# Layer 1 of a two-layer decoder: the order in which the expert units' first loads are issued, and the pace of the routing steps beside the cross-attention

## The chip, the cores and the metric

The kernel runs on one core of one Trainium2 chip. A core has TensorE (PE, matmuls; its weight loads are shown as PEld), VectorE (DVE), ScalarE (ACT), GpSimd (POOL) and SyncE (SP). In this kernel SyncE issues nearly all block loads, and GpSimd issues the indirect DMAs that send or add rows by index. The metric is the device time of one execution in microseconds (us), as the median of several runs.

## What is computed

A batch of 32 sequences of 100 tokens, 256 wide, goes through two pre-norm decoder layers. Each layer has a self-attention, a cross-attention to a context of 361 rows of 128, and a mixture of experts, each added to the residual. Layer 1, which the change touches, is this in the reference (cut):

```python
x = x + _L1_attn_ref(_layernorm(x), ...)          # linear, masked, no softmax
x = x + _L1_xattn_ref(_layernorm(x), ctx_512, ...) # 16 heads of 64, softmax over 361
x = x + _L1_ffn_ref(_layernorm(x), ...)

# _L1_ffn_ref: T = 3200 tokens, E = 64 experts, K = 8, CAP = 256
scores = sigmoid(x @ gate_weight.T)
sfc = scores + e_bias
group_scores = top_k(sfc.reshape(T, 8, 8), 2)[0].sum(-1)
_, gidx = top_k(group_scores, 4)                   # 4 of 8 groups stay
tmp = where(group is kept, sfc, 0)
_, topk_idx = top_k(tmp, 8)
topk_w = scores at topk_idx, over their sum, times 2.5
# token t takes the next free place pos of each of its 8 experts; pos >= CAP is dropped
xe[e, pos] = x[t]
h = silu(xe @ w1.T) * (xe @ w3.T)                  # per expert, 128 wide
ye = h @ w2.T
out[t] = sum over its experts of topk_w * ye[e, pos]
out = out + (silu(x @ shared_gate.T) * (x @ shared_up.T)) @ shared_down.T
```

## The kernel before

The 3200 tokens are 25 tiles of 128 rows (`NF` = 25); the residual stays in SBUF for the whole program. The order of PE's instructions is written out by hand (`manual_schedule`); for the other engines a scheduler orders the program's instructions by their dependencies and by an estimate of when they can run. DMAs on SyncE's queue are issued in that queue's order, and an instruction that has to wait holds what stands behind it on its engine.

**Cross-attention of layer 1** (`xattn_stream`, L421 to L490). It runs over `NB` = 32 sequences in 4 steps each, a step being 4 heads: 128 steps `n`, software-pipelined. In each turn of the loop PE gets the scores of step n, then what `between(n)` puts in, then the turning (transposes, L455) of the exps of step n - 1, then one `tick`, then the values (L473) of step n - 2. `between` (L853 on) puts in the projections of keys, values and queries for what comes next, and, as soon as a tile of 128 rows is whole, that tile's output projection and its norm's statistics.

**Routing beside it.** The mixture's routing can be done for a group of tiles once they are projected. `ROUTED` gives the groups: three tiles each from tile 0, 3, ..., 18 on, then two from 21 on and two from 23 on. When a group's last tile is projected, `between` appends a generator `route(f, G)` (L1576 to L1693) to `self.routes`. Between two `yield`s it does one small portion:

- the normalised rows `xr` (L191, DVE), two tiles to a portion
- the turns: transposes of `xr` on PE (L213), their copy out of the PSUM bank to `xnT` by DVE or ACT in turns; again two tiles to a portion, so a group of three has two
- the gates' matmuls (L138 with `gw`) and the sigmoid on ACT (L1599)
- eight portions on DVE, from `sfc` (L1602) by `cnt`, `gm`, `tmp`, `eq`, `sel`, `tot` and `pp` (one matmul pair on PE) to `slot` (L1681), the places of the rows
- then 8 portions per tile of the kind `SEND`: one indirect DMA of GpSimd each (L1686), 128 rows from `xr` to `x_d` in HBM by `slot`

`tick` goes over all routes and advances each by one portion, but lets only one `SEND` go per tick. A step has one tick in `between` (L889) and one after the turn, until n > 116, where `between` makes two. Inside `between`, the loop over `ROUTED` reuses the name `n` in steps in which a tile is projected, so that these steps have one tick there. What a tick adds is made to follow the work of its step (`s.after`, `lay.after`), so that it isn't brought forward.

**The end of the stream.** `last_tile` runs after the last sequence: it projects the last tile, ticks until all earlier groups are through, then routes the last group. `list1` (L1695) makes from the counts a list of the experts in the order in which they are worked (`listf`, `listi`).

**The mixture of layer 1** (`l1_ffn`, L1750 on). PE first gets the remaining portions of the shared expert that are set ahead (about 25 us of them), called the filler below. A one-element memset on GpSimd, the flag (L1784), depends on all sends. Then `units` (L1855 on) goes over the experts in the order of the list, one unit each; for unit i:

- `weights(i)` (L1860): SyncE reads the expert's number from `listi` and issues one 384 KB load to `we` (12 buffers)
- `rows(i)` (L1866): SyncE reads the list again and issues the load of the expert's rows from `x_d` to `xe` (8 buffers); it depends on the flag
- `expert_turn(i)` (L1914): transposes of `xe`, copied by ACT to `xT`
- `expert_hidden(i-1)`: the two hidden matmuls, silu on ACT, product on DVE
- `expert_add(i-2)`: the matmul back, the weight per row, and the indirect DMA that adds the rows to a sum in HBM (L1956)

Nine weights and then five rows are issued ahead of the loop; in the loop each turn issues `rows(i+5)`, then `weights(i+9)`. At the end the sums are loaded, added to the residual and written out.

Of the kernel before, what the change touches and what calls it, by code (L numbers as in the profile page):

```python
# [17 lines left out]
NB = 32  # L18
# [47 lines left out]
def tile_of(b):  # L66

    f = tiles_before(b + 1)
    return f - 1 if f > tiles_before(b) else None
# [12 lines left out]
class Kernel:  # L82
# [706 lines left out]
    def l1_xattn(self):  # L789
        nc, tc, a = self.nc, self.tc, self.a  # L790
        self.route_begin()
        with ExitStack() as st:
# [7 lines left out]
            class Lay:  # L800
# [52 lines left out]
                def between(s, n, sums):  # L853
                    b, g = divmod(n, 4)

                    part, of = {3: (0, b), 1: (1, b - 1)}.get(g, (0, -1))
                    if 0 <= of < NB:
                        r = pool.tile([T, 8], F32, tag="r", name="r")
                        nc.vector.reciprocal(r, sums[of][:, 8 * part : 8 * part + 8])
                        by_row = me.by_row(pool, r, 4)  # L860
                    if n + 1 < 4 * NB:
                        s.keys(n + 1)
                    if b < NB:
                        for c in ((0, 1), (2,))[g % 2]:
                            s.vals(b, g // 2, c)
                        if g == 0 and b + 2 < NB:
                            s.load(b + 2)
                        if b % 2 and b + 1 < NB:
                            s.queries(b + 1, 2 * g)

                    if g == 1 and 0 < b < 5:
                        f = 16 + 2 * b
                        n = min(2, NF - f)
                        me.norm_turn(f, n, me.norm_rows(f, n, bias=me.xbo1), me.bank_p())
                    if b == NB and g < 2:

                        if g == 0:
                            me.shared = me.shared1(pool.tile([P, 8, 2 * T], F32, tag="qT", name="qT"))
                        next(me.shared)
                    if b == NB and g == 2:  # L880
                        s.last_tile()
                    elif g == 2 and b > 0 and tile_of(b - 1) is not None:
                        f = tile_of(b - 1)
                        me.out_proj(f, wo)
                        me.norm_stats(f, ROUTED)
                        for f0, n in ROUTED.items():
                            if f0 + n == f + 1:
                                me.routes.append([me.route(f0, n), None])
                    for _ in range(1 + (n > 4 * NB - 12) if n < 4 * NB + 2 else 0):  # L889
                        me.tick(s.after)  # L890
                    if 0 <= of < NB:
                        s.rT = me.row_scale(pool, by_row)
# [863 lines left out]
    def l1_ffn(self):  # L1756
        nc, tc, a = self.nc, self.tc, self.a
        x = self.x
        with ExitStack() as st:
# [26 lines left out]
            whole, first, second = (0, 1), (0,), (1,)  # L1786
            units = [(u, whole) for u in range(WHOLE)] + [(u, first) for u in range(WHOLE, UNITS)]
            end = self.units(ep, units, steps)
            n = nc.values_load(self.listi[0:1, 2 * E1 : 2 * E1 + 1], min_val=0, max_val=E1)
            with tc.If(n > 0):  # L1790
                units = [(u, second) for u in range(WHOLE, UNITS)] + [(u, whole) for u in range(UNITS, E1)]
                more = self.units(ep, units)

                word = pool.tile([1, 1], F32, tag="word", name="word")
                got = nc.sync.dma_start(word, self.sum_d[0][0:1, 0:1])
                self.depend(got, [more.ins], "the units' sums")
# [57 lines left out]
    def units(self, pool, units, beside=None):  # L1854

        nc, tc = self.nc, self.tc
        we, xes, xTs, hTs, added = {}, {}, {}, {}, {}
        n_all = len(units)

        def weights(i):  # L1860
            we[i] = pool.tile([P, 768], F32, tag="we", name="we", bufs=12)
            u = units[i][0]
            e = nc.sync.value_load(self.listi[0:1, E1 + u : E1 + u + 1], min_val=0, max_val=E1 - 1)
            nc.sync.dma_start(we[i], self.a["wexp"][bass.ds(e, 1)].rearrange("o p n -> p (o n)"))

        def rows(i):  # L1866
            u, halves = units[i]
            t = xes[i] = pool.tile([P, 2, XROW], F32, tag="xe", name="xe", bufs=8)
            e = nc.sync.value_load(self.listi[0:1, u : u + 1], min_val=0, max_val=E1)
            if len(halves) == 2:  # L1870
                at = self.x1_d.rearrange("(e s p) d -> e p s d", p=P, s=2)[bass.ds(e, 1)]
                got = nc.sync.dma_start(t, at.rearrange("o p s d -> p (o s) d"))
            else:
                at = self.x1_d.rearrange("(e s p) d -> s e p d", p=P, s=2)[halves[0]][bass.ds(e, 1)]
                got = nc.sync.dma_start(t[:, 0, :], at.rearrange("o p d -> p (o d)"))
            if beside:
                self.depend(got, [self.flag.ins], "all rows are in their places")

        with tc.manual_schedule(engines={mybir.EngineType.PE}):
            room = 0.0  # L1880
            for i in range(9):
                weights(i)
            for i in range(5):
                rows(i)
            for i in range(n_all + 2):
                if i + 5 < n_all:
                    rows(i + 5)
                if i + 9 < n_all:
                    weights(i + 9)
                if i < n_all:  # L1890
                    self.expert_turn(pool, i, len(units[i][1]), xes, xTs)
                if 0 <= i - 1 < n_all:
                    self.expert_hidden(pool, i - 1, len(units[i - 1][1]), we[i - 1], xTs, hTs)

                if beside and i > 2:
                    room = room + 1.0 if i < n_all else 100.0
                    while room > 0:
                        took = next(beside, None)
                        if took is None:
                            break  # L1900
                        room -= took
                if 0 <= i - 2:
                    self.expert_add(pool, i - 2, units[i - 2], we.pop(i - 2), xes, hTs, added, beside)
        flag = pool.tile([1, 1], F32, tag="flag", name="flag_u", bufs=2)
        flag = nc.gpsimd.memset(flag, 0.0)
        self.depend(flag, added[0] + added[1], "the units' sums")
        return flag
# [174 lines left out]
```

## Time and profile before

| what | us |
|---|---|
| runs shown: median (lowest to highest, 3 runs) | 3111.43 (3109.09 to 3111.95) |
| the profiled execution's own time | 3138.55 |
| its span on the core | 3136.8 |
| mean granted clock of TensorE in it | 0.982 of full speed |
| PE busy in the span | 3002.3 |
| 1862 to 2912 | cross-attention of layer 1, up to its last steps |
| 2912 to 2944 | last steps and last tile: PE busy 25.0 of 32.0, granted clock 0.84 |
| 2944 to 2980 | list, filler, start of the units: PE busy 27.9 of 36.0 |
| 3000 to 3020 | units: PE busy 20.0 of 20.0, DMA share 0.94 |

The profiled execution is 27 us, 0.9%, above the median of the runs; durations are read from it. In a row of a timeline the two numbers are the start in the span and the duration, then come the engine, the line of the source, the operation, and what it writes and reads; "x9" says that nine neighbours are put together, and the bracket gives the idle time of the engine before it and what ended it. Line numbers are those of the kernel before.

The sends before the flag are the pieces of GpSimd's work to look for: 200 of them, 0.97 us each, 194.5 us in all. A load of weights is 384 KB, a load of rows 321 KB on the mean.

### The profile page before, as it was taken

The numbers are of one execution on the slowest core, as the hardware profiler recorded it, in microseconds if no ns is written. First come the engines' busy times: TensorE is split into PE (matmuls) and PEld (weight loads), VectorE is DVE, ScalarE is ACT, GpSimd is POOL, SyncE is SP. The second block draws the span as 40 slices with busy tenths as digits, with TensorE's granted clock in tenths as the row PEclk, the third lists the DMA queues.
The fourth block names the chain that finished last, engine by engine and source line by source line (L and its number), as shares of the span: only waits on it lengthen the run. The fifth ranks groups of instructions, "written<-read, shape, count | busy, mean of one in ns | idle before, by whom it ended". The sixth has DMA issues, their size and how long they took to land. (4 is left out here: it accounts for less than half of the span.)

```text
span 3136.8 us, 67846 instructions
## 1 busy us (share of the span) xinstructions
PE 3002.3 (96%) x26802; PEld 2251.5 (72%) x26802; DVE 1806.7 (58%) x4686; ACT 1403.8 (45%) x4361; POOL 911.1 (29%) x1040
## 2 busy tenths in 40 slices
PE   8999999999999899999998999999999999999893
PEld 7777777677777658888874677777777777776483
DVE  6666665577777632222226876666676665766354
ACT  5555554566666511122222235545555555455120
POOL 3212221465555551000015520011212112122364
PEclk9999999999999999999998999999999999999997
DMA  8860000000000033545542000010000000000296
GB/s 311 295 212 1 1 1 1 17 16 14 15 14 14 16 123 136 189 180 191 209 162 63 19 5 6 6 37 21 25 9 10 12 8 15 7 11 4 70 223 192
DMA packets 127930, 224.55 MB, mean 72 GB/s; under 512 B 39373, under 2 KB 106245, under 8 KB 120816
## 3 DMA queue, kind: packets, MB, share of 16 engines
q1 hardware_dynamic: 97680, 126.00, 12.7%
q0 software_dynamic: 26640, 90.80, 8.8%
q8 instruction: 215, 3.52, 0.5%
q10 hardware_dynamic: 3280, 3.28, 0.3%
q14 instruction: 115, 0.94, 0.1%
HBM read 152.45 MB, written 112.56 MB: 84 GB/s over the span
## 5 line engine op out<-in xcount | busy, mean ns | idle before, releaser
L1686 POOL DMA_INDIRECT x_d<-xr,slot x200 | 194.5, 972 | 773.9 <-DVE kT L133 243.6
L446 ACT ACTIVATE wBx<-ps_t,m 100x361 f32<-100x361 f32 x512 | 280.8, 560 | 258.9 <-DVE m L443 233.2
L138 PE MATMUL ps_t<-xnT,wA 128*128 128x200 f32 (+1 forms) x1600 | 328.0, 349 | 1.5 <-DMA wA<-in_wq 0.9
L138 PEld LDWEIGHTS ps_t<-xnT,wA 128*128 128x128 f32 x1600 | 271.4, 192 | 50.5 <-issue 32.2
L443 DVE TENSOR_REDUCE m<-ps_t 100x1 f32<-100x361 f32 x512 | 241.0, 525 | 78.4 <-PE ps_t L138 76.3
L138 PE MATMUL ps_t<-xT,w 128*128 128x256 f32 x1276 | 283.2, 381 | 0.7 <-ACT xT L132 0.7
L138 PEld LDWEIGHTS ps_t<-xT,w 128*128 128x128 f32 x1276 | 240.0, 190 | 41.7 <-issue 9.3
L616 DVE TENSOR_REDUCE m<-ps_t 100x1 f32<-100x361 f32 x512 | 235.4, 517 | 18.1 <-PE ps_t L138 18.1
L637 ACT ACTIVATE e<-ps_t 121x300 f32<-121x300 f32 x512 | 173.9, 426 | 123.0 <-PE ps_t L138 123.0
L340 POOL TENSOR_TENSOR e<-e,rz 100x400 f32<-100x400 f32 x128 | 109.2, 854 | 407.6 <-DVE rz L339 393.0
L336 ACT ACTIVATE e<-s,m 100x100 f32<-100x100 f32 x512 | 186.1, 365 | 21.0 <-DVE m L330 20.3
L138 PE MATMUL ps_t<-cT,wA 128*128 128x361 f32 x512 | 188.5, 492 | 1.6 <-SPq L1285 1.6
L138 PE MATMUL ps_t<-kT,qT 64*100 64x361 f32 x1024 | 189.1, 485 | 0.9 <-ACT wBx L446 0.9
L641 POOL TENSOR_TENSOR es<-e 121x400 f32<-121x400 f32 x128 | 132.2, 1033 | 197.4 <-ACT e L637 197.2
L455 PEld LDWEIGHTS ps_t<-ident,wBx 100*121 100x121 f32 x1536 | 177.9, 186 | 12.6 <-issue 5.1
L138 PE MATMUL ps_t<-wA,cT 128*121 128x512 f32 x384 | 184.9, 593 | 0.8 <-ACT wBx L446 0.8
L455 PE MATMUL ps_t<-ident,wBx 100*121 100x100 f32 x1536 | 184.8, 269 | 0.0
L138 PE MATMUL ps_t<-wA,zT 128*128 128x256 f32 x784 | 181.5, 385 | 0.0
L1367 DVE TENSOR_TENSOR h<-ps_t,g 128x256 f32<-128x256 f32 x145 | 61.2, 424 | 199.4 <-ACT g L1366 199.4
L138 PEld LDWEIGHTS ps_t<-wA,zT 128*128 128x128 f32 x784 | 147.9, 191 | 27.7 <-issue 3.3
L133 DVE COPY eT<-ps_t 121x300 f32<-121x300 f32 x339 | 146.6, 461 | 30.4 <-PE ps_t L455 26.4
L473 PE MATMUL ps_z<-eT,v 121*64 121x100 f32 x3072 | 160.9, 254 | 0.0
(317 smaller groups left out, 5741.9 us busy)
## 6 DMA issues: line engine op xcount, KB each, us to landing
x_d<-fill SPq DMA_DIRECT2D x16, 1284.0 KB
we<-in_wexp SPq DMA_DIRECT2D x32, 384.0 KB
cT<-in_ctxT SPq DMA_DIRECT2D x64, 181.5 KB
xe_d<-zero SPq DMA_DIRECT2D x8, 1024.0 KB
xe<-x_d SPq DMA_DIRECT2D x24, 321.0 KB
xe<-xe_d SPq DMA_DIRECT2D x29, 256.0 KB
y_d<-y SPq DMA_DIRECT2D x29, 256.0 KB
sum<-fill SPq DMA_DIRECT2D x10, 640.0 KB
```

The source lines that it names most:

```text
L133: return self.nc.vector.tensor_copy(out, in_)
L138: self.nc.tensor.matmul(out, lhsT=l, rhs=r, start=(i == 0), stop=(i == n - 1))
L336: nc.scalar.activation(t[:, i, :], s[:, i, :], AF.Exp, bias=m[:, i : i + 1], accum_out=rz[:, i : i + 1])
L340: nc.gpsimd.tensor_tensor(t[:, h, :], t[:, h, :], self.last(rz[:, h], T), ALU.mult)
L443: lay.after = nc.vector.tensor_reduce(m, ps[i], AX.X, ALU.max, negate=True)
L446: nc.scalar.activation(t[:, :L], ps[i], AF.Exp, bias=m, accum_out=sums[b][:, h : h + 1])
L455: nc.tensor.transpose(pt[:, c, :], e[n, i][:, c * KC : (c + 1) * KC], self.ident[:T, :T])
L473: nc.tensor.matmul(out, lhsT=v, rhs=eT[n, i][:, c, :], start=first, stop=last)
L616: nc.vector.tensor_reduce(m[:, j, o : o + 1], ps[r], AX.X, ALU.max, negate=True)
L637: nc.scalar.activation(t[:, r], ps[r].rearrange("p (c t) -> p c t", c=NKC), AF.Exp)
L641: nc.gpsimd.tensor_tensor(s, t[:, :, 0, :], t[:, :, 1, :], ALU.add)
L1686: got = nc.gpsimd.indirect_dma_start(out=self.x1_d[:, :], out_offset=bass.IndirectOffsetOnAxis(ap=slot[:, j, k : k + 1], axis=0), in_=xr[: ...
```

## The change

```diff
@@ between(), in the cross-attention of layer 1 @@
-                    for _ in range(1 + (n > 4 * NB - 12) if n < 4 * NB + 2 else 0):
+                    for _ in range(1 + (n > 2 * NB) if n < 4 * NB + 2 else 0):
                         me.tick(s.after)
@@ units() @@
             room = 0.0
-            for i in range(9):
+
+            for i in range(5):
                 weights(i)
             for i in range(5):
                 rows(i)
+                if i < 4:
+                    weights(i + 5)
             for i in range(n_all + 2):
                 if i + 5 < n_all:
                     rows(i + 5)
                 if i + 9 < n_all:
                     weights(i + 9)
```

With `NB` = 32 the second tick of `between` now comes from step 65 on, where it came from step 117 on. In `units` the same nine weights and five rows are issued ahead of the loop, in the order w0 to w4, r0, w5, r1, w6, r2, w7, r3, w8, r4, where it was w0 to w8, r0 to r4. The later loads keep their order. `units` is also called in the branch for experts beyond the planned number of units (`n > 0` in `l1_ffn`), which is there in both kernels.

## The prediction

> **What bounds the kernel now.** I read the page's busy times and slices first, then the chain of waits, then the two places the change touches: the steps of layer 1's cross-attention in which a group of tiles is routed, and the stretch in which layer 1's units begin.
>
> ```profile
> PE 3002.3 (96%) x26802; PEld 2251.5 (72%) x26802; DVE 1806.7 (58%) x4686; ACT 1403.8 (45%) x4361; POOL 911.1 (29%) x1040
> PE   8999999999999899999998999999999999999893
> ```
>
> TensorE is busy for 96% of the span, and only the slices near the end show more than a tenth of idling. So a change can gain only in the dips, and it loses wherever it puts a wait in front of a matmul. Windows cut at the step boundaries (length, then busy time of PE, PEld, DVE, ACT, POOL, the granted clock, the DMA share and GB/s):
>
> ```profile
> 2395.30:2402.66 7.36, 7.36 (x62) 5.05 (x61) 5.10 (x13) 6.43 (x18) 1.83 (x2) 1.00 0.13 34
> 2402.66:2412.30 9.64, 9.64 (x75) 7.19 (x73) 5.67 (x13) 5.99 (x16) 2.33 (x3) 1.00 0.01 2
> 2412.30:2420.14 7.84, 7.84 (x64) 5.73 (x62) 6.87 (x29) 5.25 (x13) 1.55 (x2) 1.00 0.02 2
> 2420.14:2431.91 11.77, 11.77 (x79) 8.90 (x77) 9.07 (x37) 4.02 (x12) 1.16 (x2) 1.00 0.00 0
> ...
> 2848.50:2863.32 14.82, 12.01 (x75) 8.69 (x73) 6.27 (x17) 6.00 (x15) 2.58 (x3) 0.94 0.01 1
> ```
>
> The first four rows are steps 67 to 70, where the group of tiles from 9 on is routed: TensorE is never idle, so routing is free there today. The last row is step 122, in which the two-tile group from 21 on begins: this is the one place of the trace where routing already goes at more than two ticks a step, and PE loses 2.81 us of 14.82. Two rows of PE's timeline name its waits there:
>
> ```profile
> 2860.60 0.78 PE L213 MATMUL ps_t<-ident,xr 128*128 128x128 f32 x4 [2.81 <-DVE xr L191]
> ...
> 2875.94 1.12 PE L138 MATMUL ps_t<-wA,cT 128*121 128x512 f32 x2 [0.79 <-ACT wBx L446]
> ```
>
> Together 3.60 us for that group. At the start of the units, the timelines of SyncE, GpSimd and TensorE:
>
> ```profile
> 2953.25 18.59 SPq L1864 DMA_DIRECT2D we<-in_wexp  x9
> 2972.68 6.15 SPq L1872 DMA_DIRECT2D xe<-x_d  x6
> ```
>
> ```profile
> 2963.90 0.97 POOL L1686 DMA_INDIRECT x_d<-xr,slot  x1 [0.31 <-issue]
> 2966.45 0.09 POOL L1784 MEMSET flag<- 1x1 f32 x1 [1.58 <-DMA x_d<-xr,slot]
> ```
>
> ```profile
> 2974.45 1.03 PE L138 MATMUL ps_m<-wA,wB 128*128 128x256 f32 x4
> 2976.61 0.66 PE L1914 MATMUL ps_t<-ident,xe 128*128 128x128 f32 x4 [1.13 <-DMA xe<-x_d]
> 2977.89 0.66 PE L1914 MATMUL ps_t<-ident,xe 128*128 128x128 f32 x4 [0.62 <-DMA xe<-x_d]
> 2978.38 1.89 PE L138 MATMUL ps_s<-xT,we 128*128 128x256 f32 x8
> ```
>
> The flag (every row has been sent) is up at 2966.5, but SyncE is still issuing the nine weights and reaches the first rows only at 2972.68. They land 3.9 us later, and the first expert's hidden matmul starts at 2978.38. The shared expert's filler ends at 2974.45 + 1.03 = 2975.48.
>
> **Part one: the order on SyncE.** Nothing is added or removed: the same nine weights and five rows, in another order. The chain of waits shows that the first weights cost SyncE 2.8 to 4.2 us each while GpSimd sends (the fifth is issued at 2967.43), and 1.12 us each after that (2968.15, 2969.26, 2970.38, 2971.50). So the four weights that change places cost 4 x 1.12 = 4.5 us. First rows: 2972.68 - 4.5 = 2968.2, behind the flag. Second: two weights, not four, have been moved past when its own turn comes, since a weight now stands between: 2973.84 - 3 x 1.12 = 2970.5. The fifth is where it was. Landing by the old 3.9 us: 2972.1 and 2974.4, both before the filler's end.
>
> That gain isn't had in full, because the filler is in PE's order ahead of the first turn: the turn cannot start before 2975.48. Two turns back to back at the spacing of the rows above (2976.61 to 2977.89, of which 0.62 waits) take about 1.3 us with the copy that follows, so the hidden matmul starts at about 2976.8 in place of 2978.38: **-1.6 us**. From there on TensorE is busy in full (20.00 of 20.00 us in the windows from 3000 to 3020 and from 3040 to 3060), so an earlier start reaches the end one for one.
>
> Bounds: at best the rows go as the flag rises (2972.68 - 2966.6 = 6.1 us) and land faster than 3.9 us, at 7.2 us in all by a landing 1.1 us shorter; that needs the filler out of the way. At worst SyncE is through with the nine weights before the flag (as it would be at 1.12 us each from 2949 on, done by 2960). Then the first rows, which wait for the flag, hold four weights behind them on SyncE's queue, and the later rows come one to four slots later: +1.1 to +4.5 us. I take -1.6, nearest to the rows as they are.
>
> The Trainium skill ("Perfetto Trace Analysis", section "DMA Instruction — HWDGE (DVE, Sync)") says that the DMA engines do not wait for semaphores here; the sequencer's wait comes before descriptors are made. By that rule weights six to nine stand behind the flag, which speaks against this change; with the flag at 2966.45 and the fifth weight issued at 2967.43, the trace has nothing waiting, and the rule would make the sum +1.1 to +4.5 in place of -1.6 only if SyncE were faster.
>
> **Part two: two ticks from step 65 on.** Before, the second tick in `between` came only for n > 116. Groups up to the one from 6 on are routed before step 65 and stay. Following the generator tick by tick, the groups from 9, 12, 15 and 18 on (begun at n = 66, 82, 98, 110) change; the one from 21 on and the last, in `last_tile`, tick as they did. No instruction is added. For the group from 9 on: the first turn stays in step 67, the second follows in the same `between`, the gates' matmuls come in step 67 and not 68, the DVE part from `sfc` to `slot` fills steps 68 to 71 where it filled 68 to 72, and the 24 sends end in step 80 where they ended in 85. For the last of the four, sends end in 124 in place of 126. The final 16 sends are the last group's, in `last_tile`; so the flag does not move, and this part has **no gain** to give: PE has no idle time in steps 67 to 70 to win back, and a send on GpSimd (0.97 us) has room at 29% busy.
>
> What it can cost. Both turns and the gates now fall in one step. The gates need the copy of the second turn out of its bank; that copy is in a queue behind ACT's exps or DVE's copies. By hand, from the rows of step 67, PE reaches the gates at 2401.2 and the copy ends at 2401.7: 0.5 us. Then DVE: steps 68 and 69 hold 5.67 + 6.87 = 12.54 us of DVE work in 17.48 us, of which 3.5 us is routing; at two ticks in `between` and one after the turn it becomes about 8.4 us, which gives 17.4 of 17.48. DVE has no slack left in that stretch and runs late by some 2 us; the seven transposing banks cover most of it, and I leave 0.25 us for PE. Together 0.75 us a group, four groups: **+3.0 us**. Lower bound 0: TensorE is wholly busy there, which excludes a gain. Upper bound 3.60 us a group, from the two-tile group that already goes at this pace: 4 x 3.60 = +14.4. I take a value far below it because most of that row (2.81) is a turn that waits for its own rows' DVE work in the same step, and here the rows are made one step earlier. Only the 0.79 us row is of the kind I expect. What is late next after such a wait: every matmul, since PE is in order.
>
> **Sum.** -1.6 + 3.0 = +1.4 us on the profiled execution's 3138.55 (its span is 3136.8, with 1.75 around it): 3140. This execution lies 27.1 us above the median of the runs shown, 3111.43; the slow weight issues on SyncE may be part of that, and I carry the difference over unchanged: 3111.43 + 1.4 = 3112.8, **3113 us**. A measurement of this kernel can tell about 0.2%, 6.2 us, from no change.
>
> **The rivals.** *SyncE held at the flag* (chance 0.10): if SyncE is quicker in an unprofiled run, the wait takes the place of the nine weights, as bounded above: +3.0 + 1.1 to 4.5, so 3115.5 to 3119. For it: 2.8 to 4.2 us a weight is seen only while GpSimd sends back to back. Against it: weights six to nine are needed only by experts six to nine.
>
> *Three ticks a step stall TensorE* (slower, 0.31): the four three-tile groups each lose what the two-tile group loses, 3.60 us: 14.4 - 1.6 = +12.8, **3124 us**. It decides from (6.2 + 1.6) / 4 = 1.95 us a group. For it: the only group that runs so does lose that much, and DVE gets 17.4 us of work in 17.48. Against it: its 2.81 us has a cause that the bigger groups lack, and steps 117 to 121, which have the extra tick and only sends in it, show no wait.
>
> *The filler gives way* (faster, 0.18): if the filler's own waits in this stretch (2.86 us and 2.30 us of PE idling from 2959 to 2969) are short in an unprofiled run, PE asks for the rows by 2970.3, and the early rows are worth up to 7.2 us, with routing free: 3111.43 - 7.2 = **3104 us**. Against it: whatever shortens the filler would speed up SyncE's weights as well, and then less is left to gain.
>
> *The change does nothing that counts* is inside the forecast: 40-odd sends end earlier in the middle and nobody waits for them.
>
> **How the numbers follow.** Forecast 0.41, held at the flag 0.10, stall 0.31, filler gives way 0.18. The forecast's own range is 3109 to 3118 (-1.6 alone, up to +6). Of it 0.04 is beyond +6.2, of the held case 0.03. Slower 0.31 + 0.04 + 0.03 = 0.38; faster 0.18, less 0.01 for the part of it that stays within 6.2 us; the same 0.45. The range for all: 3102, a little below the best case, to 3125, just past the stall.
>
> **What would show it.** Right: rows first issued near 2968, the hidden matmul at about 2976.8, and PE idling of 0.5 us ahead of the gates in steps 67, 83, 99 and 111, with DVE near full in the two steps after. Wrong: PE waits of 2 us and more at L213 or at scores after those steps (stall); weight six issued a slot after the flag with PE waiting for rows two to four (held); the turn at L1914 following its filler by 2971 (gives way); or a flag that moves, which would make the tick count above wrong.

## The result, and the profile after

The changed kernel takes 3115.27 us (median of 20 runs, 3111.91 to 3120.24), the kernel before 3109.72 us (20 runs, 3106.59 to 3113.99). The ratio is 1.0017, with a 95% interval from 1.0011 to 1.0023: about 5.3 us longer (0.0017 x 3109.7), inside the 0.2% that were called the same, but clear of noise at this number of runs.

```profile
span 3112.3 us, 67848 instructions
PE 2990.1 (96%) x26802; PEld 2246.0 (72%) x26802; DVE 1806.7 (58%) x4687; ACT 1404.6 (45%) x4360; POOL 913.1 (29%) x1040
```

The profile after has a *shorter* span than the profile before (3136.8), though the kernel is slower. The experiments below ran in four batches, each with the kernel before beside it; that kernel takes 3109 to 3110 us in three of them and 3140 in one. The profile before looks like that one batch: SyncE needs 18.59 us in it for nine weights, 19.2 to 19.8 in two runs of that batch, and 9.69 in a batch at 3110. What sets the batch apart is not shown; it carries the same chip number, 3, as the first batch at 3110 us. So where an expectation below speaks of a chip at 3110 or 3140 us, a batch is all that was seen, and the two profiles are not subtracted here. What can be compared is a stretch, counted from a point in it; below that point is the start of the last matmul on the last group's counts (ps_t<-acc,ones), and the stretch is list, filler and units. The kernel with the old loads that is set beside it is the one of the second experiment (ticks only), which takes the time of the kernel before and was profiled in a batch where that is 3110 us.

**SyncE.** The change's timeline (start, duration, engine, line, operation):

```profile
2925.26 5.23 SPq L1864 DMA_DIRECT2D we<-in_wexp  x5
2941.24 0.39 SPq L1872 DMA_DIRECT2D xe<-x_d  x1
2942.39 0.33 SPq L1864 DMA_DIRECT2D we<-in_wexp  x1
2943.51 0.38 SPq L1872 DMA_DIRECT2D xe<-x_d  x1
```

and that of the old order:

```profile
2925.36 9.69 SPq L1864 DMA_DIRECT2D we<-in_wexp  x9
2941.29 6.16 SPq L1872 DMA_DIRECT2D xe<-x_d  x6
```

SyncE is not slow here: nine weights take 9.69 us, where the profile before showed 18.59. In both orders the first rows leave as the flag rises (2941.1), so the new order makes them no earlier. It leaves SyncE without work from 2930.5 to 2941.2, and the second rows leave 1.1 us later, since a weight stands between.

**TensorE and VectorE.** The change, TensorE's timeline from the filler's end on (the bracket is the idle time before it and what ended that):

```profile
2943.30 1.88 PE L138 MATMUL ps_t<-xnT,wA 128*128 128x512 f32 x4
2947.64 2.08 PE L138 MATMUL ps_m<-wA,wB 128*128 128x256 f32 x4 [2.46 <-DVE x_sb L1837]
2949.51 1.64 PE L1917 MATMUL ps_t<-ident,xe 128*128 128x128 f32 x8
2951.24 1.13 PE L138 MATMUL ps_s<-xT,we 128*128 128x256 f32 x4
```

The same with the old loads:

```profile
2943.45 1.88 PE L138 MATMUL ps_t<-xnT,wA 128*128 128x512 f32 x4
2945.17 1.03 PE L138 MATMUL ps_m<-wA,wB 128*128 128x256 f32 x4
2946.03 1.04 PE L1914 MATMUL ps_t<-ident,xe 128*128 128x128 f32 x8
2947.31 1.99 PE L138 MATMUL ps_s<-xT,we 128*128 128x256 f32 x8 [0.24 <-ACT xT L1918]
```

With the change TensorE stands still 2.46 us ahead of the filler's last four matmuls, waiting for an addition on VectorE, and then takes twice as long for them (2.08 against 1.03) and longer for the first turns (1.64 against 1.04). Together that is 2.46 + 1.05 + 0.60 = 4.1 us. Why VectorE was late shows in the change's chain of waits (start, duration, what):

```profile
2943.51 3.37 DMA xe<-x_d
...
2946.90 0.35 DVE one L1949
2947.25 0.34 DVE x_sb L1837
...
2947.64 2.08 PE ps_m L138 x4
```

and in VectorE's timeline, where `one` (L1949) is the units' weight per row:

```profile
2944.07 0.35 DVE L1949 SCALAR_TENSOR_TENSOR one<-io,listf,xe 128x128 f32<-128x128 f32 x1 [7.02 <-DMA xe<-x_d]
...
2944.66 0.68 DVE L1830 TENSOR_TENSOR wB<-ps_t,wB 128x512 f32<-128x512 f32 x1
2946.90 0.35 DVE L1949 SCALAR_TENSOR_TENSOR one<-io,listf,xe 128x128 f32<-128x128 f32 x1 [1.56 <-DMA xe<-x_d]
2947.17 0.42 DVE L1837 TENSOR_TENSOR x_sb<-ps_m,x_sb 128x256 f32<-128x256 f32 x1
```

VectorE waits 7.02 us for the first rows and 1.56 us for the second, with the filler's product (L1830) and additions (L1837), whose inputs are there, queued behind. Nothing in the diff touches VectorE. But VectorE's order is the scheduler's, and it followed the loads: VectorE's program order, before and after, ends the filler like this (`-` before, `+` after, line numbers of each):

```
 L1830 wB<-ps_t,wB            hidden product of the filler
 L1837 x_sb<-ps_m,x_sb  x2    additions of the filler
+L1949 one<-io,listf,xe       first unit: needs the first rows
+L1953 by<-one
 L1830 wB<-ps_t,wB            hidden product of the filler
-L1837 x_sb<-ps_m,x_sb  x2
-L1946 one<-io,listf,xe
-L1950 by<-one
-L1946 one<-io,listf,xe
+L1949 one<-io,listf,xe       second unit: needs the second rows
+L1837 x_sb<-ps_m,x_sb  x2    (with by<-one between the two)
 L1830 wB<-ps_t,wB            last hidden product of the filler
```

The loads of rows stand earlier in SyncE's order, the scheduler puts `one` earlier in VectorE's order in turn, and on the chip the rows do not come earlier, because the flag lets none go.

**The cross-attention.** PE's groups with any idle time in front of them, from 1862 to 2900, in the change:

```profile
L138 PE MATMUL ps_t<-wA,cT 128*121 128x512 f32 x360 | 174.6, 593 | 0.9 <-ACT wBx L446 0.9
...
L213 PE MATMUL ps_t<-ident,xr 128*128 128x128 f32 x46 | 7.7, 292 | 3.1 <-DVE xr L191 3.1
```

Both are the two-tile group's, as before (0.8 and 2.8 us there). The four groups that now go at two ticks a step cost TensorE nothing.

### The profile page after: what moved, and what is told of

Read it like the earlier page. It is cut to its first block, busy times and chain, and to the rows that moved or that the text cites. A ratio compares the mean times of both kernels' runs of the same rounds, so it can differ in the third digit from the quotient of the medians.

```text
span 3112.3 us, 67848 instructions
## 1 busy us (share of the span) xinstructions
PE 2990.1 (96%) x26802; PEld 2246.0 (72%) x26802; DVE 1806.7 (58%) x4687; ACT 1404.6 (45%) x4360; POOL 913.1 (29%) x1040
## 3 DMA queue, kind: packets, MB, share of 16 engines
q8 instruction: 215, 3.52, 0.5%
```

## The experiments

In all of them the ratio is to the kernel before, run beside it in the same batch on one chip, with its 95% interval. Runs of different batches are never set against each other by their times.

### One part at a time

```diff
# order only: units() as changed, between() as before
# ticks only: between() as changed, units() as before
```

> Only the new order of loads, the ticks as before. In the profile after, SyncE is through with five weights at 2930.5 and issues nothing until the flag (2941.1), and the DMA engines stand idle from about 2934 to 2941. Theory 'idle DMA time': four weights of 384 KB are moved out of that gap into a stretch where the DMA engines are 80 to 100% busy; at the 294 GB/s of the rows from 2951 to 2961 that is 4 x 384 / 294 = 5.2 us. It expects the whole loss here: +4 to +6 us on the kernel before. Theory 'ticks' (the loss is in the cross-attention): -1.6 to +1 us.

Measured: 1.0015 [1.0006, 1.0024], 3114.72 us beside 3109.86. The whole loss is in the order of the loads, and TensorE's wait is there too (2.78 us ahead of ps_m, for x_sb).

> Only the two ticks a step, the loads in the old order. Theory 'idle DMA time': nothing, -1 to +1 us, since TensorE's matmuls of the cross-attention stand at the same distances in both profiles. Theory 'ticks': +3 us or more, as the prediction summed it (0.75 us for each of four groups).

Measured: 0.9995 [0.9986, 1.0004], 3109.72 us beside 3109.86. The pace of the routing costs nothing and brings nothing; +3.0 us would be a ratio of 1.0010, outside the interval.

### The dose: rows first, and twelve weights ahead

```diff
+            for i in range(5):
+                weights(i)
             for i in range(5):
                 rows(i)
+            for i in range(5, 9):
+                weights(i)
```

> Five weights, then the five rows, then weights six to nine; ticks as before. The rows leave as early after the flag as in the kernel before, and still four weights stand behind the flag. Theory 'idle DMA time': as slow as the new order, +4 to +6 us. Theory 'late rows' (rows two to five come one to four slots of 1.1 us later because a weight stands between): no loss, -1 to +1 us.

Measured: 1.0012 [1.0003, 1.0022], 3115.25 us (5.4 more by the medians). This went as "idle DMA time" expected and against "late rows". But its timelines show what both had overlooked: VectorE stands 7.04 us at `one`, this time with three of them ahead of the filler's work, and TensorE waits 3.29 us. From here on there was a third theory, "VectorE behind the rows".

```diff
-            for i in range(9):
+            for i in range(12):
                 weights(i)
...
-                if i + 9 < n_all:
+                if 12 <= i + 9 < n_all:
```

> The opposite dose: twelve weights (all buffers) ahead of the first rows, ticks as before; the loop then starts with the thirteenth. Twelve at 1.1 us each from 2925 are issued by 2939, still ahead of the flag. Theory 'idle DMA time': three more weights leave the busy stretch, 3 x 384 KB / 294 GB/s = 3.9 us: -2 to -4 us. Theories 'late rows' and 'ticks': no change, -1 to +1 us, or +1 to +3 us if SyncE reaches the rows after the flag.

Measured: 1.0006 [0.9997, 1.0015], 3112.01 us beside 3109.86. The gain that "idle DMA time" asked for did not come. GpSimd's timeline shows what came in its place:

```profile
2944.68 0.09 POOL L1784 MEMSET flag<- 1x1 f32 x1 [3.50 <-DMA x_d<-xr,slot]
```

The flag waits 3.50 us for the last send to land, where it waits 1.57 us with nine weights ahead (2941.17 in the run with ticks only): with the extra weights in flight (the DMA engines' share is 0.58 during this wait, and 0.02 during the one of ticks only), the last send landed 1.9 us later, and so did the first rows. VectorE did not stand in the way here, since `one` came after the filler's last addition.

### Moving VectorE's work

```diff
+        fill = the filler's last five VectorE operations
         got = nc.vector.scalar_tensor_tensor(one, ...)
+        if beside and i < 4:
+            self.depend(got, fill, "behind the filler")
```

> The changed kernel with one thing added: VectorE's weights per row (the operation on 'one') of the first four units may not stand ahead of the filler's VectorE work. Theory 'VectorE behind the rows': in the profiles of the change, of the order alone and of rows first, VectorE stands 7.0 us at 'one' for the first rows, and only then does the filler's work that TensorE waits for (2.5 to 3.3 us idle, then half the clock). Without that the loss goes: -1.5 to +1.5 us on the kernel before. Theory 'idle DMA time': four weights are still behind the flag, so the loss stays, +4 to +6 us.

Measured: 0.9988 [0.9978, 0.9998], 3135.27 us beside 3139.79: this is the batch in which the kernel before takes 30 us more than in the others. There is no loss, as "VectorE behind the rows" expected. But the change itself was not timed in this batch, so this run alone does not show that a loss went away; both were run again, below.

The opposite, on the kernel before: the last five pieces of the filler are made after the loads, and depend on `one`.

```diff
-                while us < FIRST1:
+                while us < FIRST1 - 9.6:
                     us += next(steps)
...
             for i in range(5):
                 rows(i)
+            self.ones = [one of unit 0, one of unit 1]
+            while self.us < FIRST1:
+                self.us += next(beside)   # products depend on ones[0], additions on ones[1]
```

> The kernel before, nine weights ahead of the rows, with the opposite constraint: the last five pieces of the filler have their VectorE work put behind 'one' of the first unit (the hidden products) or of the second (the additions). Theory 'VectorE behind the rows': the loss appears without any change in the loads: +2 to +5 us, with TensorE idle 1.5 to 3 us ahead of the filler's last matmuls on ps_m. Theory 'idle DMA time': -1 to +1 us.

Measured: 1.0021 [1.0012, 1.0030], 3145.51 us beside 3139.79. The loss appears with the old loads. Its timelines, VectorE and TensorE:

```profile
2980.28 0.35 DVE L1953 SCALAR_TENSOR_TENSOR one<-io,listf,xe 128x128 f32<-128x128 f32 x1 [8.28 <-DMA xe<-x_d]
```

```profile
2982.89 2.07 PE L138 MATMUL ps_m<-wA,wB 128*128 128x256 f32 x4 [3.52 <-DVE x_sb L1843]
2984.76 1.70 PE L1928 MATMUL ps_t<-ident,xe 128*128 128x128 f32 x8
```

The same picture as in the change: VectorE idle, TensorE idle (3.52 us, a little over the 1.5 to 3 expected), then matmuls at about half the pace. Not all of this profile is `one`'s doing: the execution took 3148.46 us, 3 us above the run's median, and an earlier wait of TensorE, at 2966.92, is 5.14 us long where it is 2.86 us in the profile before, with no releaser shown in either. Counted from the last matmul on the counts, the first hidden matmul is 5.8 us later than in the profile before; 2.4 us of that are there already ahead of the wait for `one`, and 3.4 us come after.

### Ten buffers for rows

```diff
-            t = xes[i] = pool.tile([P, 2, XROW], F32, tag="xe", name="xe", bufs=8)
+            t = xes[i] = pool.tile([P, 2, XROW], F32, tag="xe", name="xe", bufs=10)
```

> The kernel before with ten buffers for rows in place of eight, to look for what is left in the units: TensorE waits 4.4 us for rows in the last units of the run with ticks only, where SyncE's loads of rows wait for a buffer that a row addition still reads. If these buffers set it, most of the 4.4 us goes: -2 to -4 us. If the DMA engines or GpSimd's additions set it, -1 to +1 us.

Measured: 0.9999 [0.9990, 1.0008]. A miss for the buffers. TensorE's groups in the units show where the wait went:

```profile
L138 PE MATMUL ps_m<-we,he 128*128 128x256 f32 x112 | 29.8, 383 | 5.8 <-DVE ye L1952 2.6 <-DVE he L1932 1.9 <-SPq L1790 1.3
L1914 PE MATMUL ps_t<-ident,xe 128*128 128x128 f32 x112 | 17.6, 274 | 2.0 <-DMA xe<-x_d 2.0
```

Only 2.0 us are waited for rows, and 5.8 us at the matmuls back in their place (5.9 and 0.3 us in the profile before). What ends the units is further on; these runs do not say whether it is the chain of additions on GpSimd.

> Both: the changed kernel, 'one' of the first four units behind the filler, ten buffers for rows. By 'VectorE behind the rows' the same as ten buffers on the kernel before, within 1.5 us. By 'idle DMA time' 4 to 6 us longer than that.

Measured: 0.9991 [0.9981, 1.0002], 3137.59 us beside 3137.96 for ten buffers alone: the same, as "VectorE behind the rows" expected.

### The change, the change with `one` late, and the kernel before with `one` late, on one chip

> The changed kernel once more, beside the next two on one chip, because the run with 'one' late was on a chip on which the kernel before takes 3140 us and not 3110. Where the kernel before takes 3110 us: +4 to +6 us, as measured. Where it takes 3140 us: SyncE is slow there and reaches the first rows only 6 us after the flag in the kernel before, so the new order has something to give (the prediction's -1.6 us), less VectorE's wait: -2 to +3 us.

Measured: 1.0021 [1.0012, 1.0030], 3115.72 us beside 3108.91: the loss again, 6.8 us by the medians, a little above the range.

> The changed kernel with 'one' of the first four units behind the filler, again. Theory 'VectorE behind the rows': 3 to 6 us shorter than the changed kernel beside it, on either chip; on the kernel before -1 to +1 us where that takes 3110 us, -2 to -5 us where it takes 3140. Theory 'idle DMA time' (four weights behind the flag cost by themselves): no shorter than the changed kernel by more than 1 us.

Measured: 1.0009 [1.0000, 1.0018], 3111.43 us: 4.3 us shorter than the change beside it, as "VectorE behind the rows" expected; but 2.5 us above the kernel before, more than its ±1. TensorE's timeline shows a rest:

```profile
2951.93 0.66 PE L1924 MATMUL ps_t<-ident,xe 128*128 128x128 f32 x4 [0.77 <-DMA xe<-x_d]
2952.42 1.89 PE L138 MATMUL ps_s<-xT,we 128*128 128x256 f32 x8
2954.77 0.63 PE L1924 MATMUL ps_t<-ident,xe 128*128 128x128 f32 x4 [0.46 <-DMA xe<-x_d]
```

The second and third rows come late, with a weight ahead of each. TensorE runs at its full pace here; these two short waits were not followed by slow matmuls.

> The kernel before, nine weights ahead, with 'one' of the first four units behind the filler. In the run with ticks only VectorE stands 1.9 and 1.1 us at 'one' for the first rows and TensorE does not wait for it, so both theories expect no change: -1 to +1 us.

Measured: 1.0001 [0.9992, 1.0010], 3109.66 us. As expected, nothing: in the kernel before `one` delays nobody.

### The rest of the loss

The rows-first order of the third run, with `one` late as above.

> What is left of the loss once VectorE does not wait: the changed kernel with 'one' late was still about 2.5 us over the kernel before where that takes 3110 us, and TensorE waited 0.8, 0.5 and 0.2 us for the second and third rows, between which weights stand. Here five weights, then the five rows, then weights six to nine, 'one' of the first four units behind the filler, ticks as before. Theory 'late rows' for the rest: the first hidden matmul and the one of the ninth unit come as in the kernel before (30.5 and 60.0 us after the list's first matmul), and the time is the same, -1.5 to +1 us. Theory 'idle DMA time' for the rest: still +2 to +4 us, lost in the units after the ninth.

Measured: 1.0002 [0.9993, 1.0012], 3110.16 us beside 3108.90. TensorE's timeline is that of the old order to the hundredth:

```profile
2944.91 1.03 PE L138 MATMUL ps_m<-wA,wB 128*128 128x256 f32 x4
2945.77 1.04 PE L1923 MATMUL ps_t<-ident,xe 128*128 128x128 f32 x8
2947.05 1.99 PE L138 MATMUL ps_s<-xT,we 128*128 128x256 f32 x8 [0.24 <-ACT xT L1927]
```

The interval reaches 1.0012, 3.7 us, so by the time alone the +2 to +4 us of "idle DMA time" are not shut out. The traces show no sign of them where that theory puts them: from the ninth unit's hidden matmul to the end of the span it is 131.0 us here, and 129.8 (ticks only) and 131.8 (before, `one` late) with the old loads, one execution each. So four weights behind the flag cost nothing that these runs can tell, as long as they stand behind the rows and VectorE is free. "Idle DMA time" has nothing left to explain; the rest is "late rows".

The steps of the loss, each as a start on TensorE less the start of the last matmul on the counts (which the expectation calls the list's first matmul), in the batches where the kernel before takes 3110 us (and in the profile after):

| kernel | first hidden matmul | that of the ninth unit | ratio |
|---|---|---|---|
| ticks only (old loads) | 30.52 | 60.01 | 0.9995 |
| before, `one` late | 30.52 | 60.01 | 1.0001 |
| rows first, `one` late | 30.52 | 60.01 | 1.0002 |
| twelve weights ahead | 31.39 | 60.79 | 1.0006 |
| changed, `one` late | 31.06 | 61.58 | 1.0009 |
| changed | 34.56 | 64.05 | 1.0017 |
| changed, again | 34.56 | 64.06 | 1.0021 |
| order only | 34.88 | 65.62 | 1.0015 |
| rows first | 35.44 | 66.02 | 1.0012 |

## Why the prediction was right, and where it was wrong

The time lay in the range, and the likeliest case (no change beyond 0.2%, slightly up) came. The sum got there by luck: the order of the loads, put at -1.6 us, cost 4.9 (order only), and the ticks, put at +3.0, cost nothing.

- **"Part one: Nothing is added or removed ... -1.6."** This is the step that failed. The working took the filler's end as fixed and asked only when the rows would land. In the change the filler itself ended late, because VectorE's order changed with SyncE's: TensorE reached the first hidden matmul 4.0 us later (34.56 against 30.52), not 1.6 us earlier. The case stood in no rival. Nor was the filler's end fixed where SyncE is as slow as the working assumed. In the change with `one` late, in the batch at 3140 us, the first rows leave 26.3 us after the last matmul on the counts (30.6 in the profile before, 26.1 by the prediction's 2968.2); but TensorE waits 3.77 us for one of the filler's additions, the filler's last matmuls start 1.8 us later than in the profile before, and the first hidden matmul comes no earlier (36.30 against 36.32). The order of VectorE's instructions in both programs would have shown `one` ahead of the filler's last additions before any run.
- **SyncE's pace.** The -1.6 us rested on 2.8 to 4.2 us a weight, seen in one execution. In the profile after and in the batches at 3110 us it is 1.1 us a weight; with the old loads SyncE is through with nine at 2935 and the flag comes at 2941. (The sum for the second rows takes three weights, 3 x 1.12, which is right; the words beside it say two.) This is what the rival "SyncE held at the flag" described, and the Trainium skill's rule beside it ("Perfetto Trace Analysis", "DMA Instruction — HWDGE (DVE, Sync)": the wait is the sequencer's) fits the trace: from 2930.5 to 2941.2 SyncE issues nothing, though four weights stand ready behind the first rows. Its price, +1.1 to +4.5, holds for what is left without VectorE's wait: 0.5 us at the first hidden matmul, 1.6 us at the ninth unit, about 2.5 us in time (1.0009, from 1.0000 to 1.0018). With rows first and `one` late both starts are those of the old loads, so it is the weights between the rows; by their times alone (1.0009 and 1.0002) the two versions are not clear of each other.
- **Part two, +3.0.** Mis-sized: it measured 0 (0.9995 [0.9986, 1.0004]). TensorE waits in no step of the four groups. The tick count itself was right: the flag is 24.4 us after the last matmul on the counts in the change and with ticks only alike. VectorE's full stretch came about (in the change it is busy for 15.5 of the 16.1 us of the two steps after the turns of the group from 9 on), but TensorE is busy throughout those steps. The stall rival, 3.60 us a group, is refuted with it; its 2.81 us was the two-tile group's own, as the text had argued against it.
- **"The filler gives way"** did not come: with ticks only TensorE works through the filler's end without a gap, SyncE is quick as well, and the rows wait for the flag, as the argument against it had it.
- **Carrying 27 us over unchanged** was sound for the sum, but hid that the profile is not typical of the times. Its span is 30.2 us longer than that of ticks only; 25.3 us of that lie ahead of the last matmul on the counts and 4.9 behind it, so SyncE's slow issues can be only a small part.

What stays open: the change with `one` late was 0.9988 [0.9978, 0.9998] in the batch at 3140 us, shorter than the kernel before, yet neither its first hidden matmul nor its end comes earlier after the counts (196.4 us to the end of the span, 194.7 in the profile before). So these profiles show no gain in the units, and the change alone was not run there. Why SyncE and the filler are slower in that batch wasn't tried.

Where the kernel before takes 3110 us, no version is clearly faster. Where a load must be moved ahead, rows first with `one` late is as good as it (1.0002).

## What to carry to other kernels

Moving a load in one queue can reorder another engine where a scheduler places its instructions by when it thinks the load lands: compare every engine's order before and after, and look for an operation that needs the moved data ahead of work that is ready. A load that waits for a flag does not come earlier by being issued earlier, but everything placed by its expected landing does. Before pricing an edit by one profile, see whether its execution is typical of the times.

## What the hardware showed that was not expected

An idle gap of 2.46 us of TensorE was followed by matmuls at half pace. The change's window just after it (length, then busy time of PE, PEld, DVE, ACT, POOL, the granted clock, DMA share, GB/s), and the next:

```profile
2947.50:2951.20 3.70, 3.51 (x12) 2.81 (x12) 1.89 (x6) 0.59 (x2) 0.00 (x0) 0.56 1.01 314
2951.20:2956.00 4.80, 4.75 (x24) 4.22 (x25) 0.92 (x3) 1.93 (x4) 0.00 (x0) 1.00 0.92 308
```

The granted clock is 0.56 for 3.7 us and then full again; it adds 1.6 us to the 2.46 us of waiting. The length of a gap alone does not decide it. Two rows of TensorE in the change, 25 us earlier, and one of the kernel before:

```profile
2922.96 0.43 PE L138 MATMUL ps_t<-at,row 64*128 64x64 f32 x2 [1.18 <-DVE at L1716]
2923.50 2.08 PE L138 MATMUL ps_m<-wA,wB 128*128 128x256 f32 x4
```

```profile
2962.31 1.13 PE L138 MATMUL ps_m<-wA,wB 128*128 128x256 f32 x4 [2.86 <-issue]
```

In the change a gap of 1.18 us was enough: the granted clock is 0.57 over the next 4 us, and 0.63 after the same gap with ticks only. In the kernel before, gaps of 1.18, 2.30 and 2.86 us (ahead of 2948.33, 2969.18 and 2962.31) were followed by 4 us at 1.00. The Trainium skill ("TensorE: Matmul & The Clock Gate", section "Why this matters for your kernels") advises against idle gaps of more than about 3 us. The measurements go below the page's figure: 1.18 us were enough in one place, while 2.86 us in another were not. What decides between them these runs do not show.
